# Down stage: where the third and fourth operand wait and are split

## The chip, the cores and the metric

The kernel runs on one core of a Trainium2 chip. The core has a matrix engine (PE, with its weight loads shown as PEld), a vector engine (DVE), a scalar engine (ACT), a general engine (POOL) and a queue that issues transfers (SP). Each executes its own instructions in order and waits on semaphores for the others. The metric is the device time of one launch in microseconds, the median of several runs.

## What is computed

The reference is one transformer block on 4096 tokens of width 512, all in float32: causal linear attention, a residual and a layer norm, then a gated feed-forward part with Hadamard transforms, a residual and a layer norm. The feed-forward part, cut to what matters here:

```python
x = fwht(x * SU_ug) / SCALE
x_up = x @ W_up.T * (Wscale_ug[:INTER] * SCALE)
x_gate = x @ W_gate.T * (Wscale_ug[INTER:] * SCALE)
x = jax.nn.silu(x_gate) * x_up              # 4096 x 2048
x = fwht(x * SU_dp) / SCALE
x = x @ W_down.T * (Wscale_dp * SCALE)      # the down stage: back to 4096 x 512
```

followed by `x = _layernorm(x + ffn(x))`.

## The kernel before

**Products in three passes.** A float32 operand is split in a high half, rounded by a copy on ACT (L95), and a low half, the difference, on DVE or POOL (L96); `hilo` (L94) does both. Each product is then three matmuls: high x high, high x low, low x high. So every operand that comes from memory is loaded raw (256 KB, 128 x 512 floats), copied and subtracted before PE may use it.

**Stages.** Attention, the output projection, the gate stage and the down stage run one after the other and overlap at their borders. Gate and down stage use Strassen-like schemes with seven products instead of eight; step s is one of the seven, and `SEQ` (L701) names the PSUM bank that a step adds into.

**The gate stage** (L1020 to L1119) runs 32 rounds n, f = n // 8 being a quarter of the tokens. Each round takes seven steps, each of 12 matmuls on each of two banks, read out by `sv` (L1054) and `cc` (L1059). At a round's end POOL forms four sums (`hS`, L1119), and seven `put`s, some of them in the next round (`late_puts`), store the results to `hop_d`, from where the down stage loads them. In the last round (f = 3, p = 7) the free places between its steps are used to prepare the down stage (L1083 to L1099).

**The down stage** (L1121 to L1227) has eight units n of 512 tokens, with seven steps each. `order` holds the pairs (n, s): first (0,0), (1,0), (0,1), (1,1), (0,2) and so on, units 0 and 1 taking turns, since the weights of a step are prepared as they go; then the other units one by one. The third operand is thus (0,1), the fourth (1,1). Each pair takes 48 matmuls (L1198). `h_load` loads the four raw pieces of an operand, `h_split` makes its halves; `load_b` and `split_b` do the same for the weights B(s) of a step.

**Memory.** Tiles come from pools, and a tile that is asked for waits until the last reader of what lay there is done:
- `rp` ("ar"), 10 raw tiles: raw pieces of gate weights, operands and B;
- `wres` ("w"), 28 tiles: halves of the gate stage's weights (two per step and round), later two of the four pieces of each B;
- `yop` ("yo"), 16 tiles of twice that size: the token operands of the gate stage (`YOPS`, two per step), later the halves of (0,0) and (1,0) and the other two pieces of each B;
- `pd` ("ad"), 19 tiles, opened when the gate stage's pool `pa` is closed: the halves of all other operands. It lies where `pa` lay, with the gate stage's sums.

**Order.** The calls stand in the order written, and the framework's scheduler then moves instructions of different engines and pieces against each other by its own estimate of time; the order on each queue is fixed when the program is built. All loads and stores go through SP's queue, which holds back all that follows when a transfer has to wait.

Of the kernel before, what the change touches and what calls it, by code (L numbers as in the profile page):

```python
# [43 lines left out]
def kernel(  # L44
# [49 lines left out]
    def hilo(hi, lo, src, eng=V, pinned=False):  # L94
        i = S.activation(hi, src, AF.Copy)  # L95
        j = eng.tensor_tensor(lo, src, hi.bitcast(F32), ALU.subtract)  # L96
        if pinned:
            pin(i)
            pin(j)
# [846 lines left out]
    HR, HOP, YN, bank = {}, {}, {}, {}  # L946
    units = [(f, jp) for f in range(4) for jp in range(2)]

    def h_load(n, s):
        f, jp = units[n]  # L950
        HR[n, s] = []
        for qd in range(4):
            raw = rp.tile([128, 2, 256], F32, tag="ar", name="hraw")
            dma(raw, hop_d[f][s, jp, :, 2 * qd:2 * qd + 2])
            HR[n, s].append(raw)

# [22 lines left out]
    def y_load(n, half, pool=None):  # L979
        f, jp = units[n]  # L980
        y = pool.tile([128, 2, 512], F32, tag="yn", name="yres") if half else xtile([128, 2, 512], F32, "yres")
        for j in range(2):
            dma(y[:, j], y_d[8 * f + 2 * (2 * jp + j) + half])
        YN[n, half] = y

    def halves(xs):
        return [x[:, 2 * k:2 * k + 2] for x in xs for k in range(2)]

    def h_split_x(n, his, los):
        HOP[n, 0] = []  # L990
        for qd, raw in enumerate(HR.pop((n, 0))):
            hi, lo = his[qd], los[qd]
            hilo(hi, lo, raw, G if qd == 3 else V)
            HOP[n, 0].append((hi, lo))

    with ExitStack() as es:
        pa = es.enter_context(tc.tile_pool(name="g1", bufs=1, reuse_waits="tile"))

        def utile(name):
            return pa.tile([128, 512], F32, tag="u", name=name, bufs=16)  # L1000

        def araw(name):
            return rp.tile([128, 2, 2, 128], F32, tag="ar", name=name)

        def ff_front(i):
            y2 = []
            for e in range(2):
                y = praw.tile([128, 512], F32, tag="raw", name="y_nat")
                dma(y, y_d[2 * i + e])
                y2.append(y)  # L1010
            yield
            yield from front(i, y2, pa, lambda s, n: pgu.tile(s, F32, tag="a", name=n, bufs=4),
                             lambda s, n: pgu.tile(s, F32, tag="a", name=n, bufs=4), (ytile, xtile))

        for s in range(7):
            aload(1, s, araw("A"))
        NS = 32
        yraw, late_puts = [], []
        fr = None
        for n in range(NS):  # L1020
            f, p = divmod(n, 8)
            bank, sv, c = {}, {}, {}

            def emit(u, q, x):
                if u == 1:
                    S.activation(x, x, AF.Silu)  # L1026
                    c["g", q] = x
                else:
                    G.tensor_tensor(x, x, c.pop(("g", q)), ALU.mult)  # L1029
                    c["h", q] = x  # L1030

            if n in (1, 3, 5, 8):
                step(fr, 12)
                fr = ff_front(12 + (1, 3, 5, 8).index(n))
            new = {}
            for s, tag in enumerate(SEQ):
                first = SEQ.index(tag) == s
                wh, wl = AOP.pop((n, s))
                yh, yl = YOPS[s]
                for u in (1, 0):  # L1040
                    if first:
                        bank[tag, u] = pgu.tile([128, 512], F32, tag=tag, name="ps_" + tag, bufs=4 if tag == "a" else 2)
                    ps = bank[tag, u]
                    i = 0
                    for k in range(2):
                        for w, y in ((wh, yh), (wh, yl), (wl, yh)):
                            T.matmul(ps, w[:, u, k], y[:, k], start=first and i == 0, stop=i == 5,  # L1047
                                     skip_group_check=not first)
                            i += 1
                    it = 2 * p + (s >= 4 and s < 6)  # L1050
                    sc = wsc[:, u, it:it + 1]
                    if s in (0, 2, 4):
                        x = pa.tile([128, 512], F32, tag="sv", name="sv", bufs=6)
                        S.activation(x, ps, AF.Copy, scale=sc)  # L1054
                        sv[s, u] = x
                    if s in (1, 4, 6):
                        src, k, q = {1: (ps, 0, 0), 4: (bank.get(("b", u)), 4, 3), 6: (ps, 2, 1)}[s]
                        x = utile("cc")
                        V.scalar_tensor_tensor(x, src, sc, sv[k, u], ALU.mult, ALU.add)  # L1059
                        emit(u, q, x)  # L1060
                    if s == 5:
                        if u == 1:
                            x = utile("sg")
                            S.activation(x, ps, AF.Silu, scale=sc)
                            c["g", 2] = x
                        else:
                            x = c.pop(("g", 2))
                            V.scalar_tensor_tensor(x, ps, sc, x, ALU.mult, ALU.mult)
                            c["h", 2] = x
                if n and s in (1, 2, 3):  # L1070
                    for _ in range(3):
                        if late_puts:
                            late_puts.pop(0)()
                if n + 1 < NS:
                    asplit(n + 1, s)
                if n + 2 < NS:
                    aload(n + 2, s, araw("A"))
                if p == 7:
                    if f < 3:
                        new[s] = ysplit(s, yraw[s])  # L1080
                        if s < 5:
                            yraw.append(yload(f + 1, s + 2))
                    elif s == 0:  # L1083
                        hx = [praw.tile([128, 2, 256], F32R, tag="raw", name="hxh") for _ in range(3)]
                        hx.append(wres.tile([128, 2, 256], F32R, tag="w", name="hxh"))
                        hy = [ytile([128, 4, 256], F32R, x) for x in ("hxl", "hxl", "hxh", "hxh", "hxl", "hxl")]
                        h_split_x(0, hx, halves(hy[0:2]))
                        h_load(1, 0)
                        y_load(0, 0)
                        y_load(1, 0)  # L1090
                    elif s == 2:
                        split_b(0)
                        load_b(1)
                    elif s == 3:
                        h_split_x(1, halves(hy[2:4]), halves(hy[4:6]))
                        load_b(2)
                    elif s == 4:
                        split_b(1)
                        h_load(0, 1)  # L1099
                elif n == NS - 2:  # L1100
                    if s == 4:
                        h_load(0, 0)
                    elif s == 6:
                        load_b(0)
                step(fr)
            if p == 6 and f < 3:
                yraw = [yload(f + 1, 0), yload(f + 1, 1)]
            YOPS.update(new)
            H = {"A11": c["h", 0], "A12": c["h", 2], "A21": c["h", 1], "A22": c["h", 3]}

            def put(key, f=f, p=p, H=H):
                dma(hop_d[f][WKEY.index(key)].rearrange("j p i t -> p j i t")[:, :, p],
                    H[key].rearrange("p (j t) -> p j t", j=2))

            late_puts = [lambda k=k, put=put: put(k) for k in ("A11", "A12", "A22", "S1", "S3", "S2", "S4")]
            for key, x0, x1, op in (("S1", "A21", "A22", ALU.add), ("S3", "A11", "A21", ALU.subtract),
                                    ("S2", "S3", "A22", ALU.subtract), ("S4", "A12", "S2", ALU.add)):
                H[key] = utile("h" + key)
                G.tensor_tensor(H[key], H[x0], H[x1], op)  # L1119

    with ExitStack() as es:  # L1121
# [36 lines left out]

        todo = None
        for idx, (n, s) in enumerate(order):  # L1160
            if 0 < idx and idx + 1 < len(order):
                h_split(*order[idx + 1])
            if n == 0 and s + 2 < 7:
                split_b(s + 2)
            if 0 < idx and idx + 2 < len(order):
                h_load(*order[idx + 2])
            if n == 1 and s + 3 < 7:
                load_b(s + 3)
            for put in late_puts[:3]:
                put()  # L1170
            late_puts = late_puts[3:]
# [113 lines left out]
```

## Time and profile before

| | us |
|---|---|
| median of 3 runs | 2294.09 (2293.67 to 2295.06) |
| the profiled execution | 2294.93 |
| its span | 2293.2 |
| PE busy in the span | 2253.7 |
| DVE, ACT, POOL busy | 1760.5, 1393.9, 1282.8 |
| PE busy, 1800 to 1900 us (gate stage) | 100.00 of 100 |
| PE busy, 1900 to 2000 us (from gate to down stage) | 94.76 of 100 |
| PE busy, 2000 to 2100 us | 98.43 of 100 |
| PE busy, 2100 to 2200 us | 100.00 of 100 |

PE is the busiest engine nearly everywhere, so what counts is where it stands still and for whom. Times in the profile are us from the span's start. In a line of a view, `out<-in` are the names of tiles: `hraw` is a raw piece of an operand, `hah` and `hal` its halves in `pd`, `hxh` and `hxl` its halves elsewhere, `braw` a raw piece of B, `wdh`, `wdl` and `wdzh`, `wdzl` the halves of B, `ps_da`, `ps_db`, `ps_dc` the banks of the down stage. "SPq" is the SP queue issuing a transfer. The granted clock is the share of PE's full clock.

### The profile page before, as it was taken

Reading aid. Unit: us, or ns where it says so; the run is one execution under the profiler, and the core shown is the slowest. Engines: PE = TensorE matmul, PEld = TensorE weight load, DVE = VectorE, ACT = ScalarE, POOL = GpSimd, SP = SyncE. Lnnn points to the kernel's source line nnn. Section 1 sums busy time; section 2 is a strip of 40 time slices with the busy share of each in tenths; the row PEclk is TensorE's granted clock in tenths of the full one; section 3 lists DMA queues with packets and bytes.
Section 4 is the critical chain, followed back from the end, with each engine's and each line's share of the span. In section 5 each row is a group of like instructions: output and inputs, shape, how many; then the busy total and the mean of one; then the engine's idle time right before and its main releaser. Section 6 shows DMA issues by size and latency. Waiting matters only on the chain. (4 is left out here: it accounts for less than half of the span.)

```text
span 2293.2 us, 42225 instructions
## 1 busy us (share of the span) xinstructions
PE 2253.7 (98%) x14432; PEld 2000.2 (87%) x14432; DVE 1760.5 (77%) x2684; ACT 1393.9 (61%) x2515; POOL 1282.8 (56%) x1063
## 2 busy tenths in 40 slices
PE   8999999999999999899999999999999999999998
PEld 7999999899999998688878878878788888899998
DVE  8888888888888889688898775766866756675555
ACT  7777777777777777444443566655655555464553
POOL 5556666555555556478787445565555555633332
PEclk9999999999999999999999999999999999999999
DMA  6665665555555554989987976876765767887773
GB/s 197 177 180 170 181 181 172 168 156 151 165 160 159 167 159 137 323 265 272 283 285 258 308 247 212 254 234 191 236 205 188 241 186 208 253 277 236 227 251 121
DMA packets 369527, 484.15 MB, mean 211 GB/s; under 512 B 68670, under 2 KB 224384, under 8 KB 365344
## 3 DMA queue, kind: packets, MB, share of 16 engines
q1 hardware_dynamic: 369312, 481.45, 68.6%
q8 instruction: 114, 1.87, 0.3%
q14 instruction: 101, 0.83, 0.1%
HBM read 282.76 MB, written 156.76 MB: 192 GB/s over the span
## 5 line engine op out<-in xcount | busy, mean ns | idle before, releaser
L288 PE MATMUL ps_qk<-xh,wh 128*128 128x256 f32 x1280 | 355.1, 277 | 0.0
L288 PE MATMUL ps_qk<-xl,wh 128*128 128x256 f32 x1280 | 354.9, 277 | 0.0
L288 PE MATMUL ps_qk<-xh,wl 128*128 128x256 f32 x1280 | 354.4, 277 | 0.0
L394 POOL TENSOR_SCALAR_AFFINE_SELECT A<-A 64x512 fp32r<-64x512 f32 x256 | 212.3, 829 | 240.9 <-DVE am L390 144.5
L1029 POOL TENSOR_TENSOR cc<-cc 128x512 f32<-128x512 f32 x96 | 149.3, 1558 | 287.3 <-ACT cc L1026 136.7
L96 DVE TENSOR_TENSOR wol<-A,woh 128x512 fp32r<-128x512 f32 x217 | 223.1, 1035 | 103.8 <-ACT woh L95 91.9
L270 POOL TENSOR_TENSOR sw<-sw,csb 128x512 f32<-128x512 f32 x160 | 208.7, 1304 | 134.2 <-ACT sw L269 116.2
L288 PEld LDWEIGHTS ps_qk<-xh,wh 128*128 128x128 f32 x1280 | 240.5, 188 | 3.1
L288 PEld LDWEIGHTS ps_qk<-xh,wl 128*128 128x128 f32 x1280 | 240.4, 188 | 0.9
L288 PEld LDWEIGHTS ps_qk<-xl,wh 128*128 128x128 f32 x1280 | 240.5, 188 | 0.3
L95 ACT ACTIVATE woh<-A 128x512 fp32r<-128x512 f32 x217 | 135.4, 629 | 134.1 <-PE ps_b L1047 76.8
L95 ACT ACTIVATE hah<-hraw 128x512 fp32r<-128x512 f32 x216 | 133.5, 629 | 125.5 <-PE ps_da L1198 60.3
L96 POOL TENSOR_TENSOR hal<-hraw,hah 128x512 fp32r<-128x512 f32 x78 | 107.6, 1384 | 177.6 <-PE ps_da L1198 71.7
L1047 PE MATMUL ps_a<-yoh,woh 128*128 128x512 f32 x512 | 202.7, 397 | 1.3 <-ACT sv L1054 0.9
L1047 PE MATMUL ps_a<-yol,woh 128*128 128x512 f32 x512 | 202.4, 395 | 0.0
L1047 PE MATMUL ps_a<-yoh,wol 128*128 128x512 f32 x512 | 199.8, 396 | 0.0
L96 DVE TENSOR_TENSOR hal<-hraw,hah 128x512 fp32r<-128x512 f32 x138 | 107.6, 788 | 98.3 <-PE ps_da L1198 30.9
L173 PE MATMUL ps_wo<-wh,oh 128*128 128x512 f32 x372 | 147.8, 397 | 2.5 <-ACT oh L95 2.5
L1054 ACT ACTIVATE sv<-ps_a,wsc 128x512 f32<-128x512 f32 x192 | 127.0, 680 | 37.7 <-PE ps_a L1047 37.5
L173 PE MATMUL ps_wo<-wh,ol 128*128 128x512 f32 x372 | 147.6, 397 | 0.0
L173 PE MATMUL ps_wo<-wl,oh 128*128 128x512 f32 x372 | 147.3, 396 | 0.0
L271 DVE TENSOR_TENSOR ps_qk<-ps_qk,csb 128x512 f32<-128x512 f32 x160 | 111.2, 695 | 31.9 <-ACT sw L269 31.1
(280 smaller groups left out, 7352.1 us busy)
## 6 DMA issues: line engine op xcount, KB each, us to landing
hraw<-hop_d SPq DMA_DIRECT2D x224, 256.0 KB
vd<-vhl SPq DMA_DIRECT2D x128, 256.0 KB
num_d<-num SPq DMA_DIRECT2D x128, 256.0 KB
rb<-rec_d SPq DMA_DIRECT2D x128, 256.0 KB
hop_d<-hS SPq DMA_DIRECT2D x128, 256.0 KB
nt<-num_d SPq DMA_DIRECT2D x31, 1024.0 KB
A<-in_wug_dram SPq DMA_DIRECT2D x93, 256.0 KB
hop_d<-cc SPq DMA_DIRECT2D x64, 256.0 KB
```

Source lines behind the costliest of these rows:

```text
L95: i = S.activation(hi, src, AF.Copy)
L96: j = eng.tensor_tensor(lo, src, hi.bitcast(F32), ALU.subtract)
L173: T.matmul(ps, l[:, h], r, start=i == 0, stop=i == 47)
L270: G.tensor_tensor(sw, sw, sinb, ALU.mult)
L271: V.tensor_tensor(ps, ps, cosb, ALU.mult)
L288: T.matmul(ps[:, j], W[key][wa][:, k * 128:(k + 1) * 128], B[xa][:, k], start=i == 0, stop=i == 11)
L394: G.affine_select(ah, ah.bitcast(F32), pattern=[[0, 8], [1, 64]], compare_op=ALU.is_ge, fill=0.0, base=0, channel_multiplier=-1)
L1029: G.tensor_tensor(x, x, c.pop(("g", q)), ALU.mult)
L1047: T.matmul(ps, w[:, u, k], y[:, k], start=first and i == 0, stop=i == 5, skip_group_check=not first)
L1054: S.activation(x, ps, AF.Copy, scale=sc)
```

## The change

1. `h_load` can take its raw tiles from another pool. The raw pieces of (0,1) and (1,1) go into `wres`, and are loaded in the last gate round after steps 1 and 3. Before, (0,1) was loaded into `rp` after step 4, and (1,1) at the second pair of the down stage.
2. The halves of (0,1) go into four tiles of `yop` instead of `pd`, made at the first pair of the down stage instead of the second, and all four low halves are formed on DVE; before, two of the four were on POOL.
3. The loads and splits of B move: `load_b(2)` from after step 3 to after step 4 of the last gate round; in the down stage `split_b(s + 2)` from unit 0's pairs to unit 1's, and `load_b` of the same step from unit 1's pair before to unit 0's.
4. At the second pair, (1,1) is split and (0,2) is loaded; before, (0,1) was split and (1,1) loaded there. At the third pair nothing is split or loaded of the operands. From the fourth pair on these two calls are as before.

```diff
-    def h_load(n, s):
+    def h_load(n, s, pool=None, tag="w"):
         f, jp = units[n]
         HR[n, s] = []
         for qd in range(4):
-            raw = rp.tile([128, 2, 256], F32, tag="ar", name="hraw")
+            raw = (rp if pool is None else pool).tile([128, 2, 256], F32, tag="ar" if pool is None else tag, name="hraw")
             dma(raw, hop_d[f][s, jp, :, 2 * qd:2 * qd + 2])
             HR[n, s].append(raw)
...
-    def h_split_x(n, his, los):
-        HOP[n, 0] = []
-        for qd, raw in enumerate(HR.pop((n, 0))):
+    def h_split_x(n, his, los, s=0):
+        HOP[n, s] = []
+        for qd, raw in enumerate(HR.pop((n, s))):
             hi, lo = his[qd], los[qd]
-            hilo(hi, lo, raw, G if qd == 3 else V)
-            HOP[n, 0].append((hi, lo))
+            hilo(hi, lo, raw, G if qd == 3 and s == 0 else V)
+            HOP[n, s].append((hi, lo))
...
                         y_load(1, 0)
+                    elif s == 1:
+                        h_load(0, 1, wres)
                     elif s == 2:
                         split_b(0)
                         load_b(1)
                     elif s == 3:
                         h_split_x(1, halves(hy[2:4]), halves(hy[4:6]))
-                        load_b(2)
+                        h_load(1, 1, wres)
                     elif s == 4:
                         split_b(1)
-                        h_load(0, 1)
+                        load_b(2)
...
         for idx, (n, s) in enumerate(order):
-            if 0 < idx and idx + 1 < len(order):
+            if idx == 0:
+                hy = [ytile([128, 4, 256], F32R, x) for x in ("hxh", "hxh", "hxl", "hxl")]
+                h_split_x(0, halves(hy[0:2]), halves(hy[2:4]), 1)
+            elif idx == 1:
+                h_split(*order[3])
+            elif 2 < idx and idx + 1 < len(order):
                 h_split(*order[idx + 1])
-            if n == 0 and s + 2 < 7:
+            if n == 0 and 0 < s and s + 2 < 7:
+                load_b(s + 2)
+            if n == 1 and s + 2 < 7:
                 split_b(s + 2)
-            if 0 < idx and idx + 2 < len(order):
+            if idx == 1:
+                h_load(*order[4])
+            elif 2 < idx and idx + 2 < len(order):
                 h_load(*order[idx + 2])
-            if n == 1 and s + 3 < 7:
-                load_b(s + 3)
```

## The prediction

> **What bounds the kernel now.** I read the page's head and engine shares first: the sum is made against this execution.
>
> ```profile
> span 2293.2 us, 42225 instructions
> PE 2253.7 (98%) x14432; PEld 2000.2 (87%) x14432; DVE 1760.5 (77%) x2684; ACT 1393.9 (61%) x2515; POOL 1282.8 (56%) x1063
> ```
>
> TensorE (PE) is busy for 2253.7 of 2293.2 us. The change issues no more and no fewer matmuls, so it can only move what PE loses: 39.5 us in all. The second view is PE's own waits, longest first (in total, times, longest):
>
> ```profile
> PE ps_v L241 <- ACT wh L95: 5.7, 2, 4.9
> PE ps_dc L1198 <- DVE hal L96: 5.2, 1, 5.2
> PE ps_num L414 <- ACT num L418: 2.6, 2, 1.8
> ```
>
> The first belongs to the kernel's start. The second is one wait of 5.2 us, in the down stage, and the change edits just there. The chain of work that ended last shows what led up to it (start, us, what):
>
> ```profile
> 1959.40 0.64 ACT wdh L95
> 1960.05 0.02 issue
> 1960.07 0.70 DVE wdl L96
> 1960.77 0.02 issue
> 1960.79 3.71 DMA braw<-wdop_d
> ...
> 1965.23 1.31 POOL wdzl L96
> 1966.54 2.46 POOL hS L1119 x2
> 1969.00 0.02 issue
> 1969.01 2.18 DMA hop_d<-hS
> ...
> 1972.27 14.10 PE ps_dc L1198 x94
> 1986.37 11.41 PE ps_da L1198 x96
> ```
>
> Read it downwards: the weights of step 3 are loaded, split, loaded, split; behind that split POOL forms the gate stage's last sums (hS); their store frees memory that the split of operand (0,1) writes into; only then may PE begin ps_dc. PE had nothing from 1967.0 to 1972.3. The last two lines show a second loss: 94 matmuls of ps_dc took 14.10 us where 96 of ps_da took 11.41. Stretches around the gap (length, busy us of PE, PEld, DVE, ACT, POOL, then granted clock) say why:
>
> ```profile
> 46.28:49.70 3.42, 1.44 (x7) 0.96 (x7) 3.36 (x5) 2.60 (x5) 2.37 (x3) 1.00 0.21 77
> 49.70:53.11 3.41, 3.41 (x17) 3.24 (x16) 3.41 (x7) 2.03 (x4) 1.47 (x2) 0.50 0.00 0
> 961.06:964.47 3.41, 1.63 (x10) 1.11 (x9) 2.44 (x9) 2.44 (x5) 1.27 (x2) 1.00 1.03 312
> 964.47:967.89 3.42, 3.42 (x17) 2.74 (x16) 3.06 (x5) 3.15 (x8) 1.02 (x2) 1.00 0.92 361
> 1967.99:1971.40 3.41, 0.00 (x0) 0.00 (x0) 0.00 (x0) 0.63 (x1) 3.25 (x3) 1.00 0.72 223
> 1971.40:1974.82 3.42, 2.55 (x12) 2.55 (x13) 3.41 (x3) 3.12 (x6) 3.42 (x3) 0.50 0.80 237
> ```
>
> After the idle stretch the granted clock is 0.50. It is also 0.50 after a stretch with PE busy 1.44 of 3.42 us, but stays 1.00 after 1.63 of 3.41.
>
> So the price of the wait is 5.2 us idle plus 14.10 - 94 x 11.41 / 96 = 2.9 us at half clock: **8.1 us**. That is the most this change can win here.
>
> **The change, part by part.** The profiled execution took 2294.93 us (span 2293.2 and 1.7 around it), the median of the runs shown is 2294.09; I apply the difference found to the median. The order of each queue in the changed kernel is fixed when it is built, so I read it there; the durations are all from before. (n,s) is unit n, step s; B(s) are the weights of a step.
>
> *Raw pieces of (0,1) and (1,1) in weight tiles.* Eight loads of 256 KB are issued earlier: (0,1)'s before B(1)'s last pieces, (1,1)'s among B(1)'s and B(2)'s. The number of DMAs is the same. On SP's queue each now also waits for PE to release a gate weight tile, and the gate's stores and B(1)'s loads queue behind them. B(1)'s last piece was issued at 1925.20 and would move back by about the eight issues and their waits, some 7 us by my walk down the queue; its split came at 1947 to 1951 and it is needed with (0,1) at 1967.0. Hidden: 0 us. If that cover went, the gate's stores would come late first.
>
> *Halves of (0,1) in token tiles, DVE for all four.* The split no longer writes into the gate's memory, so it no longer waits for the store of hS. Its own wait is for the token tiles, which the gate's late steps read until 1958.8 at most; with four copies of 0.63 us on ACT and four subtractions of 0.69 to 1.74 us on DVE it is done by 1964, 3 us ahead of 1967.0. Two subtractions go from POOL (1.30 us each) to DVE (0.69): off the path. So PE runs on at 1967.0: **-8.1 us**, all of the loss.
>
> *What is late next: (1,1).* The 48 matmuls of (0,1) take 5.71 us ("PE ps_db L1198 x48" and its like in the chain), so PE wants (1,1) at 1972.7. Its halves still go to the memory that the gate's sums free, and on ACT its copies now stand behind four copies of B(4), whose split was far later before. B(4)'s ladder: its first load needs a raw slot that POOL's last subtraction of B(3) frees; B(3) is split into token tiles of the gate's last step, free at 1959.2. From there: ACT's evacuation and the copies of B(2) to 1961, then two POOL subtractions of 1.30 to 1.75 us: first load issued at about 1963.9. Pieces 3 and 4 land in the slots of pieces 1 and 2, so load, copy, subtract, load, copy follow one another, exactly as B(3) does above. Price of such a ladder from first issue to the last copy's start:
> - upper end, as B(3)'s whole ladder ran: first issue 1952.82, last copy 1964.52, 11.7 us;
> - lower end: two loads of 3.43 (issue 1958.84 to copy 1962.27) and 3.71, a copy of 0.64, two subtractions of 0.69 and 0.61: 9.1 us;
> - taken: 10.9, nearer the upper, because POOL's hS sums run at the same time and a DVE subtraction beside POOL takes up to 1.74.
>
> Then 0.54 for that copy and 0.63 for the first of (1,1): PE can start at 1963.9 + 10.9 + 1.2 = 1976.0, between 1974.2 and 1976.8. Idle 3.3 us, ends 1.5 and 4.1. The second product of halves needs DVE's subtraction, 0.7 to 1.2 us after the copy: another 1.0. **+4.3 us** (2.5 to 5.1).
>
> *The clock at the new gap.* By the rows, a stretch of 3.41 us with under about 1.5 us of PE work is followed by half clock. If the stretches lie as in this trace, 1971.40 to 1974.82 holds 1.3 us of work: half clock follows, for one or two stretches. Lower end 0 (the gap falls across two stretches), upper end the 2.9 paid before. Taken **+1.4**: two chances in three of about 2.1, since the later waits of (1,1) hide part.
>
> [...]
>
> *The wait added in the gate.* ACT's copy of B(3)'s first piece now stands ahead of a gate evacuation (sv, L1054) and waits for its load. The bank is wanted again by PE near 1957. Ends: 0 (the load is early) and 1.5 us (the load takes 5.91 us as one "hraw<-hop_d" in the chain at 2053, not 4.14 as the "braw<-wdop_d" at 1955). Taken **+0.4**, near the 4.14.
>
> *B(2) onwards.* split_b one unit later, load_b one unit ahead of it: the same copies, 28 DMAs, the same 11.4 us per step to hide in: 0. The stall of 1.6 us at 2060 ("PE ps_da L1198 <- DVE yres L1208") is queued alike in both and stays.
>
> Sum: -8.1 + 4.3 + 1.4 + 0.4 = **-2.0 us**. Ends: -8.1 + 2.5 = -5.6 and -8.1 + 5.1 + 2.9 + 1.5 = +1.4. 2294.09 - 2.0 = 2292.1.
>
> **The rivals.**
> - *The gap all but closes* (faster). If B(4)'s ladder runs at its lower end and the gap splits over two stretches, the loss is 2.5 us or less: 2294.09 - 5.6 = 2288.5. For it: stores ran at 2.18 us or so in this stretch once loads were few. Against: (1,1) still shares POOL and DVE with hS.
> - *ACT's queue becomes the bound* (slower). ACT executes in order, and loads now stand ahead of both the gate's evacuation and (1,1). If three loads on that path take 5.91 us instead of 3.7, the two in the ladder add 4.4 and the one in the gate 1.5 to 2.2: loss 4.3 + 4.4 + 2.9 + 2.0 = 13.6 against 8.1, 2299.6. The kernel falls behind before from about 4.4 us per load (three times 0.7 uses up the 2.0), and by over 0.2% from about 5.4 (three times 1.7 and the other 1.5 of clock). Against: the loads in the chain here took 3.71 to 4.14.
> - *It does not do what it says*: the token tiles are freed so late that (0,1) still waits. It would take 3 us more than worked out; the wait then stays where it was: 2294.
>
> **How the numbers follow.** Moved wait, as summed: 0.66, 2292.1 with its own ends 2288.5 to 2295.5. Gap closed: 0.16. ACT bound: 0.10. No effect: 0.08. 0.2% is 4.6 us, about what a measurement of this kernel can tell from no change. Faster by more: most of the closed gap and a little of the moved wait, 0.18. Slower by more: the ACT bound and little else, 0.11. Same: 0.71. The range leaves out the far half of each outer case: 2288.4 to 2296.6.
>
> **What would show it.** Right: PE's wait on "ps_dc <- DVE hal" at 1967 gone, a new one at ps_dc near 1973 to 1976 of 2 to 4 us, released by ACT hah or DVE hal, with ACT waiting for "braw<-wdop_d" just before; a half-clock stretch behind it. Wrong: PE without a wait between 1960 and 1990 (then my ladder is too slow), or a wait of ps_a L1047 over 1 us near 1957, or new waits after 1990.

## The result, and the profile after

| | before | after |
|---|---|---|
| median, us | 2295.28 (22 runs) | 2298.74 (22 runs) |
| profiled execution, us | 2294.93 | 2299.26 |
| its span, us | 2293.2 | 2297.5 |
| PE busy in the span, us | 2253.7 | 2258.4 |

The changed kernel takes 1.0016 times as long (95% interval 1.001 to 1.0021), some 3.5 us more. That is still within 0.2%, but the forecast was 2.0 us less; its median lies above the range, 2288.4 to 2296.6. Part of the miss is the base: the three runs of before that the forecast started from had a median of 2294.09, all 22 have 2295.28. With the range moved up by those 1.2 us, 2298.74 would still lie above it.

PE's busy time rose too, though the matmuls are the same in number: a matmul at half clock counts as busy for longer (18 are in a stretch of 3.42 us at half clock below, 31 in the one at full clock from 1988.14; from one start to the next it is 0.21 us against 0.12). The prediction's "it can only move what PE loses: 39.5 us" left that out.

First PE's own waits between 1900 and 2100 us of the changed kernel (us in total, times, longest):

```profile
PE ps_dc L1207 <- ACT hah L95: 4.9, 1, 4.9
PE ps_da L1207 <- DVE yres L1217: 0.9, 1, 0.9
PE ps_a L1047 <- ACT sv L1054: 0.9, 1, 0.9
PE ps_dc L1207 <- DVE hal L96: 0.6, 1, 0.6
PE ps_b L1047 <- DVE cc L1059: 0.5, 1, 0.5
```

Before, this stretch had one wait of 5.2 us at ps_dc behind DVE hal, for operand (0,1), and one of 1.6 us behind yres. The wait for (0,1) is gone, and the one behind yres is down to 0.9 us. In the place of the first stand 4.9 + 0.6 = 5.5 us for (1,1), and 0.9 + 0.5 = 1.4 us of new waits in the gate stage (ps_a, ps_b).

What led to the 4.9 us is in the chain of work that ended last (start, us, what):

```profile
1968.55 1.72 DVE wdzl L96
1970.29 3.98 DMA braw<-wdop_d
...
1974.28 0.65 ACT wdh L95
...
1974.95 1.35 DVE wdl L96
1976.32 4.79 DMA braw<-wdop_d
...
1981.67 0.62 ACT hah L95
...
1982.37 1.31 DVE hal L96
...
1983.72 6.38 PE ps_dc L1207 x35
```

Subtract, load, copy, subtract, load, copy: this is the ladder of B(4), and the first copy of (1,1) (hah) comes right behind it. ACT's timeline says the same from the other side (start, us, operation, in brackets the idle time before it and what ended that):

```profile
1973.01 0.63 ACT L95 ACTIVATE wdh<-braw 128x512 fp32r<-128x512 f32 x1 [6.59 <-DMA braw<-wdop_d]
1974.28 0.64 ACT L95 ACTIVATE wdh<-braw 128x512 fp32r<-128x512 f32 x1 [0.64 <-DMA braw<-wdop_d]
1977.94 0.63 ACT L95 ACTIVATE wdzh<-braw 128x512 fp32r<-128x512 f32 x1 [3.02 <-DMA braw<-wdop_d]
1981.13 0.63 ACT L95 ACTIVATE wdzh<-braw 128x512 fp32r<-128x512 f32 x1 [2.56 <-DMA braw<-wdop_d]
1981.67 1.65 ACT L95 ACTIVATE hah<-hraw 128x512 fp32r<-128x512 f32 x3
```

From 1966.4 to 1981 ACT does little but wait for weights, and `hah` behind them waits too.

The stretches around the gap (length, busy us of PE, PEld, DVE, ACT, POOL, then granted clock, share of the DMA engines, GB/s):

```profile
1974.48:1977.90 3.42, 2.96 (x25) 2.76 (x23) 2.04 (x3) 0.44 (x1) 1.26 (x1) 1.00 0.49 146
1977.90:1981.31 3.41, 0.00 (x0) 0.00 (x0) 0.69 (x1) 0.80 (x2) 0.00 (x0) 1.00 0.90 255
1981.31:1984.72 3.41, 1.79 (x6) 1.50 (x7) 2.35 (x3) 3.41 (x7) 2.88 (x2) 0.50 0.77 208
1984.72:1988.14 3.42, 3.42 (x18) 3.42 (x17) 3.42 (x3) 2.76 (x6) 3.42 (x3) 0.50 0.72 243
```

One stretch is wholly idle; the two behind it run at half clock, with 1.79 + 3.42 = 5.21 us of PE work in them. 22 matmuls start there (the second row also counts two that began in the first), which at full clock, where 48 take 5.71 us, would need 2.6 us: the other 2.6 are lost.

The new loss in the changed place is thus 1.4 + 5.5 + 2.6 = 9.5 us, against 5.2 + 2.9 = 8.1 before: +1.4 us (the wait behind yres, 0.7 us shorter, is not counted in this). The same can be read without a model. From the start of the 11600th matmul of the profile (near 1922 us, before anything that the change moves is waited for by PE) to that of the 14400th, the kernel before took 360.38 us and the changed one 361.64: +1.3. The other 3.1 us between the two profiles lie before the 11600th matmul, in work that the change leaves alone: there half clock was granted for 3.4 us in all in the profile of before (one stretch, near 50 us), and for 17.1 us in that of the changed kernel (near 50 us, and three stretches between 909 and 944 us). So two profiles show where 1.3 us came from; the medians differ by 3.5.

### The profile page after: what moved, and what is told of

The parts are those of the page before. It is cut to its first block, busy times and chain, and to the rows that moved or that the text cites. A ratio compares the mean times of both kernels' runs of the same rounds, so it can differ in the third digit from the quotient of the medians.

```text
span 2297.5 us, 42223 instructions
## 1 busy us (share of the span) xinstructions
PE 2258.4 (98%) x14432; PEld 2004.4 (87%) x14432; DVE 1769.1 (77%) x2686; ACT 1392.8 (61%) x2515; POOL 1280.0 (56%) x1061
## 4 chain that ended last, share of the span: by engine, by line
PE 89%; DMA 4%; DVE 3%; ACT 2%; issue 1%; POOL 0%; SPq 0%; DVEq 0%; ACTq 0%; POOLq 0%
PE ps_qk L288 17%; PE ps_a L1047 15%; PE ps_wo L173 13%; PE ps_da L1207 8%; PE ps_b L1047 7%; PE ps_num L414 6%; PE ps_s L337 4%; PE ps_v L241 4%; PE ps_db L1207 4%; PE ps_c L1047 4%; PE ps_dc L1207 2%; PE ps_sc L380 1%; PE ps_sc L381 1%; PE ps_den L415 1%; DMA rb<-rec_d 1%
## 5 line engine op out<-in xcount | busy, mean ns | idle before, releaser
L96 POOL TENSOR_TENSOR hal<-hraw,hah 128x512 fp32r<-128x512 f32 x76 | 103.0, 1358 | 177.3 <-PE ps_da L1207 75.2
```

## The experiments

Theory A: the wait for (1,1) is set by ACT's order, its copies standing behind the ladder of B(4); the stores of the gate's last sums (hS), whose memory the halves of (1,1) take, come second. Rival R: those stores set it, as they set the wait for (0,1) before. Theory G, formed from the result: the gate's new waits come from weights that the early raw pieces pushed back. The measure beside the median is the time from the 11600th to the 14400th matmul, which leaves out what happened earlier. "Gate" is the waiting at ps_a and ps_b, "gap" that at ps_dc, both between 1900 and 2100 us.

| kernel | gate, us | gap, us | half clock at the gap, us | 11600th to 14400th, us | median against before (95%) |
|---|---|---|---|---|---|
| before | 0 | 5.2 | 6.8 | 360.38 | 1 |
| before, second profile | 0 | 5.0 | 6.8 | 359.34 | |
| after | 1.4 | 5.5 | 6.8 | 361.64 | 1.0016 (1.001 to 1.0021) |
| after, second profile | 1.1 | 5.1 | 6.8 | 360.86 | |
| const_hS | 1.0 | 5.3 | 6.8 | 361.76 | 1.0009 (1.0 to 1.0018) |
| b4_later | 1.5 | 2.6 | 0 | 356.23 | 0.999 (0.9979 to 1.0) |
| tok_only | 0 | 1.5 | 0 | 355.92 | 0.9977 (0.9968 to 0.9986) |
| raw_only | 1.0 | 7.6 | 6.8 | 365.96 | 1.0028 (1.0015 to 1.0041) |
| tok_h11w | 0 | 0 | 0 | 357.04 | 0.9986 (0.9977 to 0.9995) |
| h11_w_b4 | 1.3 | 0 | 0 | 353.38 | 0.9985 (0.9976 to 0.9994) |
| b2_first | 0 | 6.2 | 6.8 | 360.62 | 0.9997 (0.9988 to 1.0006) |
| tok_h11w_b4 | 0 | 0 | 0 | 355.38 | 0.9968 (0.9956 to 0.998) |

### The store of hS replaced (const_hS)

In the last gate round the four sums are still formed, but the stores send a constant tile in their place, so that no store waits for the sums or reads their memory. Part of the output is therefore not the reference's.

```diff
-                    H[key].rearrange("p (j t) -> p j t", j=2))
+                    (wsdp if H is last and key[0] == "S" else H[key]).rearrange("p (j t) -> p j t", j=2))
```

(`last` is the last round's H.)

> The changed kernel, but in the last gate round the four sums hS are formed and not stored; a constant tile of the same size is stored in their place, so part of the down stage's input is wrong. The number of transfers is the same, but no store reads the gate's memory of hS any more, and no store waits for POOL. Theory A (the wait of (1,1) is ACT's queue: the copies of B(4), waiting for B(4)'s loads, stand ahead of it): PE's wait at ps_dc for ACT hah stays at 3.5 to 5.5 us, the time stays within 2.5 us of the changed kernel's 2298.7. Rival R (the halves of (1,1) wait for the stores of hS to free the gate's memory, as (0,1) did before): the wait falls under 1 us, half clock goes with it, and the time falls by 6 to 8 us to 2291 to 2293.

Measured: 4.4 + 0.9 = 5.3 us at the gap, as in the changed kernel, and 2297.45 us. ACT's timeline of this kernel:

```profile
1973.12 0.63 ACT L95 ACTIVATE wdzh<-braw 128x512 fp32r<-128x512 f32 x1 [3.37 <-DMA braw<-wdop_d]
1976.13 0.63 ACT L95 ACTIVATE wdzh<-braw 128x512 fp32r<-128x512 f32 x1 [2.38 <-DMA braw<-wdop_d]
1976.66 5.82 ACT L95 ACTIVATE hah<-hraw 128x512 fp32r<-128x512 f32 x11
```

The copies of (1,1) start at the very end of B(4)'s last copy, with no store to wait for. R falls: the stores alone do not set this wait.

### B(4) and later weights one unit later (b4_later)

The changed kernel with the loads and splits of the weights moved back:

```diff
-            if n == 0 and 0 < s and s + 2 < 7:
-                load_b(s + 2)
-            if n == 1 and s + 2 < 7:
-                split_b(s + 2)
+            if n == 0 and s == 1:
+                load_b(3)
+            if n == 1 and s < 2:
+                split_b(s + 2)
+            if n == 1 and 0 < s and s + 3 < 7:
+                load_b(s + 3)
+            if n == 0 and 1 < s and s + 2 < 7:
+                split_b(s + 2)
```

> The changed kernel with B(4) and later weights loaded and split one pair later, so that the split of (1,1) stands ahead of B(4) on ACT. Theory A: PE's wait at ps_dc for (1,1) falls from 4.9 us to 1 to 2.5 us, mostly without half clock, and the time falls by 4 to 6 us to 2292.5 to 2295. Rival R (memory freed by the stores): the wait stays at 4 to 5 us and the time at 2297 to 2300.

Measured: 2293.29 us, 2.6 us at the gap (just above what was expected), no half clock. With the ladder out of the way, the chain ahead of the gap is another:

```profile
1971.08 1.75 POOL hS L1121
1972.86 3.76 DMA hop_d<-hS
...
1976.74 1.73 DVE hal L96
...
1978.51 4.51 PE ps_dc L1211 x36
```

Now it is the store of hS that ends last. So A's order holds: ladder first, store next.

### One half of the change alone (tok_only, raw_only)

tok_only is the kernel before with the halves of (0,1) in token tiles (and `h_split_x` as in the change, part 2), made at the second pair; raw pieces and weights are loaded and split as before:

```diff
...
-            if 0 < idx and idx + 1 < len(order):
+            if idx == 1:
+                hy = [ytile([128, 4, 256], F32R, x) for x in ("hxh", "hxh", "hxl", "hxl")]
+                h_split_x(0, halves(hy[0:2]), halves(hy[2:4]), 1)
+            elif 1 < idx and idx + 1 < len(order):
                 h_split(*order[idx + 1])
```

> The kernel before with one part of the change alone: the halves of (0,1) in token tiles; raw pieces stay in the raw pool and are loaded when they were. Theory A: the harm of the change comes from the early raw pieces, which let B(4) overtake (1,1) on ACT and put a load ahead of a gate evacuation; without them PE waits at most 1 to 2 us at ps_dc for (1,1), not at all at ps_a and ps_b L1047 near 1958, and the time is 4 to 6 us under the kernel before (2289 to 2291). Rival (the wait only moves, whatever is done with the raw pieces): PE waits 4 to 5 us at (1,1) and the time is that of before, 2295, or above.

Measured: 2290.86 us, 1.5 us at the gap behind the store of hS, nothing in the gate. This part alone wins 5 us.

raw_only is the rest of the change: the changed kernel with the halves of (0,1) in `pd` as before:

```diff
-                hy = [ytile([128, 4, 256], F32R, x) for x in ("hxh", "hxh", "hxl", "hxl")]
-                h_split_x(0, halves(hy[0:2]), halves(hy[2:4]), 1)
+                h_split(*order[2])
```

> The changed kernel with the other part alone: raw pieces of (0,1) and (1,1) early in weight tiles, but the halves of (0,1) in the pool that lies on the gate's memory, as before. Theory A: the ladder of loads now stands ahead of (0,1): PE's wait at ps_dc is 6 to 7.5 us with half clock behind it, the waits in the gate near 1958 stay, and the time is 1 to 4 us above the changed kernel (2300 to 2303). Rival (the early raw pieces do no harm, it is the token tiles): no wait in the gate, 5.2 us at ps_dc as before, 2295.

Measured: 2301.83 us, 7.0 + 0.6 = 7.6 us at the gap and 1.0 us in the gate. The sizes are about as expected, and the rival falls, but the chain doesn't say what made the wait at the gap:

```profile
1970.70 1.39 POOL hS L1121
1972.09 3.68 DMA hop_d<-hS
...
1975.79 0.62 ACT hah L95
```

ACT's timeline has the last copy of the weights just ahead of it:

```profile
1975.26 0.63 ACT L95 ACTIVATE wdzh<-braw 128x512 fp32r<-128x512 f32 x1 [1.83 <-DMA braw<-wdop_d]
```

The store of hS landed at 1975.8, and the copy ended at 1975.26 + 0.63 = 1975.9: both at once. This run shows what the early raw pieces, with the moved weights, cost without the token tiles, not by which of the two ways. From the 11600th to the 14400th matmul they cost 365.96 - 360.38 = 5.6 us; the changed kernel takes 361.64 - 355.92 = 5.7 us more than tok_only. So the two halves of the change add up: -4.5 and +5.6.

### Weights before raw pieces again (b2_first)

The changed kernel with B(2) loaded after step 3, as before, and (1,1) after step 4:

```diff
-                        h_load(1, 1, wres)
+                        load_b(2)
                     elif s == 4:
                         split_b(1)
-                        load_b(2)
+                        h_load(1, 1, wres)
```

> The changed kernel with the raw pieces of (1,1) loaded one step later and the weights B(2) one step earlier, as before; all else as changed. Theory G (the gate's waits, 1.4 us in the changed kernel at ps_a and ps_b, come from weights whose loads the raw pieces pushed back: ACT's copy of B(3)'s first piece and DVE's splits stand ahead of the gate's evacuations): the waits at ps_a and ps_b between 1900 and 2100 us fall to under 0.5 us in all, and the wait at ps_dc stays or grows by about as much, since PE arrives earlier and the ladder of B(4) does not move: 4.5 to 6.5 us, so 2296 to 2299 us all the same. Rival (the gate's waits come from the split of (0,1) into token tiles, DVE being full beside POOL): 1.0 to 1.5 us stay at ps_a and ps_b, and the wait at ps_dc is as in the changed kernel, 4.5 to 5.5 us.

Measured: no wait in the gate, 5.6 + 0.6 = 6.2 us at the gap, 2296.07 us, the same as before. All as G expected: the gate's waits come from the order of two groups of loads, the raw pieces of (1,1) and B(2), in the queue.

In the changed kernel two things stood ahead of the gate's evacuations. ACT's `sv` stood behind the copy of B(3)'s first piece, which waited 1.52 us for its load, and two copies of (0,1):

```profile
1958.90 0.64 ACT L95 ACTIVATE wdh<-braw 128x512 fp32r<-128x512 f32 x1 [1.52 <-DMA braw<-wdop_d]
1959.44 1.14 ACT L95 ACTIVATE hxh<-hraw 128x512 fp32r<-128x512 f32 x2
1960.48 0.66 ACT L1054 ACTIVATE sv<-ps_a,wsc 128x512 f32<-128x512 f32 x1
```

And `cc` on DVE stood behind a row of subtractions:

```profile
1949.16 1.78 DVE L96 TENSOR_TENSOR wdl<-braw,wdh 128x512 fp32r<-128x512 f32 x1
1950.87 1.79 DVE L96 TENSOR_TENSOR hxl<-hraw,hxh 128x512 fp32r<-128x512 f32 x1
1952.58 1.78 DVE L96 TENSOR_TENSOR wdl<-braw,wdh 128x512 fp32r<-128x512 f32 x1
1954.28 1.77 DVE L96 TENSOR_TENSOR wdzl<-braw,wdzh 128x512 fp32r<-128x512 f32 x1
1955.97 1.40 DVE L1059 SCALAR_TENSOR_TENSOR cc<-ps_c,wsc,sv 128x512 f32<-128x512 f32 x2
```

In b2_first the same row ends at 1950.64 instead of 1955.97, and `sv` goes at 1954.31 instead of 1960.48; PE runs 3.5 us earlier in that profile, so the two come 1.9 and 2.7 us sooner for it.

### The halves of (1,1) out of the gate's memory (tok_h11w, h11_w_b4, tok_h11w_b4)

Three kernels with the halves of (1,1) in the gate's idle weight tiles, so that they too don't wait for the store of hS. The edit in the first, over tok_only (in the second, two of these lines, `hw` and `h_split_x`, replace the split of (1,1) at the second pair):

```diff
...
+            elif idx == 2:
+                hw = [wres.tile([128, 2, 256], F32R, tag="w", name=x) for x in ("hxh",) * 4 + ("hxl",) * 4]
+                h_split_x(1, hw[0:4], hw[4:8], 1)
-            elif 1 < idx and idx + 1 < len(order):
+            elif 2 < idx and idx + 1 < len(order):
```

> The kernel before with the halves of (0,1) in token tiles and, new, those of (1,1) in gate weight tiles; raw pieces and weights as before. With the first part alone the one wait left at the gap was 1.5 us at ps_dc, and the chain ahead of it ran through the last store of hS (landed 1975.8), whose memory (1,1)'s halves take. Theory A (the memory freed by the store holds (1,1), B(4) is split late enough): that wait goes to under 0.5 us, no half clock between 1960 and 1990, 2288.5 to 2290.5 us. Rival (POOL and DVE are too busy there, whatever the memory): 1 to 2 us stay at ps_dc behind DVE hal, 2290 to 2292 us.

Measured: no wait at ps_dc any more, but 2292.31 us, above what was expected, and no better than tok_only. New waits of 1.8 and 0.9 us came at ps_da for (0,2), one operand on, and those behind yres grew to 3.0 us. Its chain has the ladder of B(4) there:

```profile
1974.40 4.03 DMA braw<-wdop_d
...
1978.99 0.62 ACT hah L95
...
1979.64 1.36 DVE hal L96
...
1981.04 10.96 PE ps_da L1204 x90
```

The second is the changed kernel with this and with the weights of b4_later:

> The changed kernel with both late things taken away: B(4) and later weights one pair of units later, and the halves of (1,1) in gate weight tiles. Each alone left a wait at ps_dc (2.6 us with only the weights later; 4.4 us with the stores of hS replaced). Theory A (B(4)'s ladder first, the store of hS next, nothing third): under 0.8 us left at ps_dc, the gate's waits at ps_a and ps_b stay at 1.0 to 1.5 us since the splits stand ahead of the gate's last evacuations as in the changed kernel, 2290 to 2292.5 us. Rival (a third wait takes the place: DVE's subtractions are late): 1.5 to 3 us at ps_dc behind DVE hal, 2292.5 to 2294.5 us.

Measured: 2291.97 us, 0.2 us left for operands in the whole stretch, 1.3 us in the gate. Its profiled execution, 2287.0, was the fastest of its 11 runs, so its 353.38 us flatter it.

The third is tok_h11w with the ladder one unit later:

```diff
-            if n == 0 and s + 2 < 7:
-                split_b(s + 2)
+            if n == 0 and s == 0:
+                split_b(2)
+            if n == 1 and s == 0:
+                load_b(3)
+            if n == 0 and s == 1:
+                split_b(3)
...
-            if n == 1 and s + 3 < 7:
-                load_b(s + 3)
+            if n == 0 and s > 1 and s + 2 < 7:
+                load_b(s + 2)
+            if n == 1 and s > 1 and s + 2 < 7:
+                split_b(s + 2)
```

> The kernel before with the halves of (0,1) in token tiles, those of (1,1) in gate weight tiles, and B(4) and later weights one unit later; raw pieces of (0,1) and (1,1) as before. Without the last part the gap at ps_dc was gone, but 1.8 and 0.9 us of waiting came at ps_da for (0,2), behind ACT's copy hah with a load of weights just ahead of it, and 3.0 us at ps_da behind yres. Theory A (that wait is B(4)'s ladder once more, one operand on): it falls to under 0.5 us, no half clock between 1960 and 2060, 2288 to 2291 us, the fastest of the study. Rival (another transfer, of the operand itself, takes its place): 1.5 to 3 us stay at ps_da, 2291 to 2293 us.

Measured: 2290.16 us, 0.9968 times before: the lowest median of the study (its interval overlaps that of tok_only). No wait for an operand is left between 1900 and 2100 us; what is left are two waits of 2.5 and 2.1 us behind yres:

```profile
PE ps_da L1210 <- DVE yres L1220: 4.6, 2, 2.5
```

### Both kernels once more (after_again, before_again)

> The changed kernel once more, for a second profile of it. Theory A: the wait at ps_dc is again 3.5 to 6 us and released by ACT hah, the gate's waits at ps_a and ps_b again 1 to 2 us, half clock between 1974 and 1990 for 3.4 or 6.8 us. The stretch of half clock at about 49 us, in the kernel's start, which the change does not touch, may be 3.4 or 6.8 us: if it varies between profiles of the same kernel, part of the difference between the two first profiles is no effect of the change.

> The kernel before once more, for a second profile of it. Theory A: the wait at ps_dc for (0,1) is again 4.5 to 6 us and released by DVE hal behind the store of hS, with one stretch of half clock of 3.4 us behind it. From the start of the matmul that is the 11600th of each profile to that of the 12000th (just past the gap), the changed kernel should take 1 to 3 us longer in this pair of profiles too.

Measured: the second profile of after has 4.5 + 0.6 us at the gap and 1.1 us in the gate; that of before has 5.0 us for (0,1). Half clock lasted 6.8 us in both, as in the first profile of before too: "one stretch of 3.4" was wrong. From the 11600th to the 12000th matmul the changed kernel took 2.0 us longer in the first pair (74.11 against 72.14) and 1.7 in the second (72.80 against 71.09), both within what was expected; at the 14400th 1.3 and 1.5 are left.

The time up to the 11600th matmul is 1921.66 and 1925.68 us for before, 1924.72 and 1922.98 for after. It varies by up to 4 us between profiles of the same kernel, with no order between the two. The time at half clock ahead of that matmul goes with it in these four: 3.4 and 17.1 us for before, 17.1 and 10.2 for after; over all twelve profiles the two go together less closely. (The single times of these second profiles, 2297.91 us for before and 2296.76 for after, stand the other way round than the medians.)

## Why the prediction was wrong

**The step that failed** is the price of what was put ahead. The prediction set the early raw pieces at "Hidden: 0 us", and its three added terms at 4.3 + 1.4 + 0.4 = 6.1 us. The runs show 5.5 + 2.6 + 1.4 = 9.5 us, more than the 8.1 that the token tiles win; and all that was done beside the token tiles costs 5.6 to 5.7 us from the 11600th to the 14400th matmul (raw_only, tok_only). That accounts for some 1.3 of the 3.5 us by which the median rose; the rest stays open, as said below.

**That the wait for (0,1) goes: right.** The 5.2 us are gone in every kernel with the token tiles, and in tok_only, where little takes their place, 5 us are won. The price of that wait with its half clock, 8.1 us, fits too: tok_h11w_b4, which has neither a gap nor half clock there, passes the gap 8.2 us sooner (63.93 us from the 11600th to the 12000th matmul, against 72.14).

**That (1,1) is late next, behind B(4)'s ladder on ACT: right in mechanism, too small in size.** The term was +4.3 (2.5 to 5.1), measured 5.5. The ladder's first load was issued at 1968.49, the last copy started at 1981.13: 12.6 us, where 10.9 was taken and 11.7, B(3)'s whole ladder, held for the upper end. The loads took 4.5, 4.0 and 4.8 us, the middle subtraction 1.35. And the ladder began later: 1968.49 less the 3.1 us by which this profile ran behind is 1965.4, not 1963.9. That the ladder sets the wait is shown by const_hS (no store of the sums, the wait stays) and b4_later (no ladder ahead, half of the wait goes); what is left there is the store's.

**The clock: +1.4 forecast, 2.6 measured**, near the upper end of 2.9. The lower end was the hope that the gap falls across two stretches. b4_later's 2.6 us fell so (2.46 and 1.75 us of PE work in its two stretches, clock 1.00); this one of 4.9 us held a whole stretch. In the second profile of after falling across two stretches did not help: 4.5 us left 1.36 and then 0.80 us of PE work in two stretches, and half clock followed for 6.8 us all the same. No run with a gap this long reached the lower end of 0.

**The gate's wait: +0.4 forecast, 1.4 measured**, near the upper end of 1.5. Here a step was wrong: of the raw pieces in weight tiles the prediction said "Hidden: 0 us", and asked only whether B(1) is split in time for its own use. It is; but the loads and splits of B(2) and B(3) behind it slid into the gate's last evacuations, on ACT and on DVE, and PE waited for those. b2_first gives the price: with one pair of loads exchanged, the gate's waits go, and the median is that of before (0.9997, 0.9988 to 1.0006). The gap grows by 0.7 us meanwhile, since PE comes earlier to a ladder that ends no earlier by as much.

**The sum.** With the measured terms it reads -8.1 + 5.5 + 2.6 + 1.4 = +1.4: the upper end of the likeliest case, as it was put down. The ladder came out beyond its upper end (5.5 against 5.1), the other two just below theirs. For the ladder and the clock a shared cause is plain: of these runs, those with a gap of 5.0 us or more at ps_dc all had 6.8 us of half clock there, those with 2.6 or less none, so here the longer gap paid twice. That the early pieces also tie the gate's wait to the other two was not shown; in b2_first it went while they stayed. The stall behind yres, which the prediction took to stay, shrank by 0.7 us (by 0.2 in the second pair of profiles).

**The rivals.** "ACT's queue becomes the bound" has the right sign and the right place, loads that stand ahead of both the gate's evacuation and (1,1). It needed more than 4.4 us per load for the changed kernel to fall behind: the two loads in the ladder's chain took 4.0 and 4.8 us, the one in the gate 5.3 (issued at 1953.63, copied at 1958.90). The 5.9 us that 2299.6 was worked out from were not reached, and the 0.5 us of the gate's wait behind DVE it left out. "The gap all but closes" and "it does not do what it says" did not come about.

**"B(2) onwards: 0": not shown.** No run moves the weights' loads and splits of the down loop (part 3) by themselves; raw_only and tok_only only divide the token tiles from all the rest.

**What stays open.** The two pairs of profiles put 1.3 and 1.5 us in the changed place; the medians of 22 runs differ by 3.5 (by the interval, 0.001 to 0.0021 of 2295.28, 2.3 to 4.8). The rest was not found in a profile. One pattern points to the gate. In the five kernels with waits there (after, const_hS, b4_later, raw_only, h11_w_b4) the median stands 0.2 to 3.2 us higher against before than the time from the 11600th to the 14400th matmul does; in the four without them (tok_only, tok_h11w, b2_first, tok_h11w_b4) it stands 0.1 to 1.6 us lower (each by one profile; the second profiles of before and after differ from the first by 1.0 and 0.8 us). So by the medians the exchange of loads in b2_first is worth more than the 1.0 us of the profiles (2298.74 is 3.5 us above its before, 2296.07 0.6 below). That the changed place costs more in other executions, for instance where a short wait in the gate takes a stretch of half clock with it, would fit, but none of the profiles shows it. Nor was it tried to slow one load of the ladder by itself.

## What to carry to other kernels

When work is put ahead on a queue, price not only the moved work but everything that now runs behind it, down to where the queue's next consumer waits: here a "free" early load cost more in the gate than expected (1.4 us against 0.4), and exchanging two groups of loads took it away again. When one uncertain term goes with another, as here the length of the gap at ps_dc with the half clock there (5.0 us and more: 6.8 us of it; 2.6 and less: none), their upper ends come together; adding up the middles is then too hopeful. And of a change with several parts, run each alone: here the token tiles alone won 0.2%, and the rest, early raw pieces and moved weights, took it back.

## What the runs showed of the hardware

A wait of 2.0 us cost clock. In tok_only, PE waited that long for yres; the stretch that held the wait, and the next two (columns as above):

```profile
2053.49:2056.90 3.41, 1.45 (x13) 1.25 (x11) 0.69 (x1) 0.63 (x1) 0.52 (x1) 1.00 0.90 325
2056.90:2060.32 3.42, 3.38 (x16) 3.38 (x17) 1.85 (x3) 0.41 (x1) 0.00 (x0) 0.50 1.05 403
2060.32:2063.73 3.41, 3.41 (x30) 3.41 (x30) 0.82 (x2) 1.49 (x3) 0.74 (x1) 1.00 1.02 362
```

With 1.45 us of work in 3.41 the next stretch ran at half clock: 16 matmuls, where the one behind it at full clock has 30. At 5.71 us for 48, as at full clock before and after the change, 16 would take 1.9 of the 3.38 us, so by this estimate at least 1.5 us is lost on top of the wait. On the way back, 1.79 us of work in a half-clock stretch did not bring the full clock in the changed kernel, 3.38 us did here.

The busy share of a stretch did not settle it. The prediction read from two rows that less than about 1.5 us of PE work costs clock. But in the changed kernel a stretch at 906.11 with 2.66 us of work (in the attention) was followed by clock 0.50 too, and so was one at 926.59 with 1.69; a stretch with 1.63 us, at 961.06, kept the full clock in the kernel before. So the bound does not hold over the whole kernel, and what makes the difference was not tried.

DVE and POOL were slower side by side. The subtractions in the changed kernel's DVE timeline above start every 1.70 us; POOL's operations in the same stretch do too:

```profile
1950.36 1.75 POOL L96 TENSOR_TENSOR hxl<-hraw,hxh 128x512 fp32r<-128x512 f32 x1
1952.07 1.74 POOL L1121 TENSOR_TENSOR hS<-hS,cc 128x512 f32<-128x512 f32 x1
1953.76 1.74 POOL L96 TENSOR_TENSOR wdzl<-braw,wdzh 128x512 fp32r<-128x512 f32 x1
1955.46 1.75 POOL L1121 TENSOR_TENSOR hS<-sg,hS 128x512 f32<-128x512 f32 x1
```

Alone, the same DVE subtraction took 0.69 us (at 1959.57, POOL idle), and POOL's of `wdzl` 1.30 (at 1953.91 in the kernel before, DVE idle). So beside POOL's operations each subtraction on DVE, at 1.77 to 1.79 us, took two and a half times as long. The two subtractions that the change moves from POOL to DVE met little of this: the four of (0,1), all on DVE now, took 1.29 us (from 1960.18) and 1.73 us (from 1963.30) for two each, near the 0.69 us apiece that the prediction took.
